# Eighteen batches of x rows, an earlier index load and a later far flag in a graph layer's edge loop

## The chip, the core and the metric

The kernel runs on one core of one Trainium2 chip. A core has a matrix engine (PE), a vector engine (VectorE, DVE in the profile), a scalar engine (ScalarE, ACT), GpSimd (POOL), a queue engine (SyncE, SP) and 16 DMA engines. The metric is the device time of one execution in microseconds. It is the median of several runs.

## The reference, cut to what matters

12500 nodes have rows x of 160 floats, 400000 edges have a source, a target (sorted by target), 16 and 4 attributes.

```python
h = jnp.maximum(_layernorm(x, axis=-1), 0.0)
# inside the layer, node_input is h, node_attr is node_vec1 (a)
s0 = x0 @ W_sc0 * a * inv0                 # skip path, 64 scalars
s1 = jnp.einsum('nuc,uv->nvc', x1, W_sc1) * a[:, :, None] * inv1
y0 = x0 @ W_l1_0 * a * inv0                # the rows that edges gather
y1 = jnp.einsum('nuc,uv->nvc', x1, W_l1_1) * a[:, :, None] * inv1
hid = jax.nn.silu(edge_length_embedded @ fc_W1 * (1.0 / math.sqrt(FC_IN)))
w = hid @ fc_W2 * (1.0 / math.sqrt(FC_H))  # 192 weights per edge, w_a w_b w_c w_d
ys0 = y0[edge_src]
ys1 = y1[edge_src]
mid_a = w_a * ys0 * e0                     # and mid_b, mid_c, mid_d: products of w, ys and e
z0 = jnp.zeros((n, MID), mid0.dtype).at[edge_dst].add(mid0) * inv_nb
z1 = jnp.zeros((n, MID, 3), mid1.dtype).at[edge_dst].add(mid1) * inv_nb
o0 = z0 @ W_l2_0 * a * inv_mid
o1 = jnp.einsum('nuc,uv->nvc', z1, W_l2_1) * a[:, :, None] * inv_mid
out = x + concat(C_S * s0 + C_X * o0, C_S * s1 + C_X * o1)
```

## The kernel before

**Node stage.** The nodes are 98 tiles of 128 rows, in groups of 2, then 8, and at the end 4 and 4. SyncE loads groups of x into `acc` (`load_x`, L322), which is also the accumulator of the output. Step q (two tiles) runs through `moments`, `center`, `turn_rows`, `out_of_psum`, `map_rows` and `leave`, each some steps later. ScalarE writes the rows y of a group into a buffer `ys` of the pool `ny` (two buffers), and SyncE stores it to `y_d` in DRAM. A buffer can be written again only when its store is done. On the engines the instructions stand in the order in which the code names them (a manual schedule), so an engine that waits holds up all that stands behind.

**Gathers.** An edge tile is 128 edges, a batch four tiles; there are 3125 tiles in 782 batches. For each tile GpSimd issues one indirect DMA that fetches 128 rows of y by the edges' sources (`gather`, L565). It can start only when all of `y_d` is stored. Batch b + 4's first gather is also held until the sums of batch b are done on PE, the third one of batch b + 3 until half of batch b's are (a dependency put in by hand, L576).

**Batches of x rows.** Every 16th batch, from batch 19 on, and 16 of them in all (`XB`), takes no rows from `y_d`. Its rows of x are gathered during the node stage (`x_fetch`, L345, into `xr`, by indices `xi` that `x_index` loads) and turned into rows of y in the edge loop (`hot`, `look_up`, `pick`, `x_center`, `x_turn`, `x_map`, `x_scale`). In the node stage each of these gathers is tied to an earlier step's `map_rows`.

**Edge loop.** For batch b: PE computes the edge weights two batches ahead (`weigh`, L599), VectorE the products of the next batch (`products`, L614, with a selection matrix `sel`), PE the sums over targets (`sums`, L626; four `pz` products per batch, two PSUM buffers that VectorE's transposes empty). A group of four windows then goes through `linear`, `add` and `accumulate` (L664, VectorE adds into `acc`). The list `waiting` holds up to two VectorE steps, which run at the start of the next batch (L867).

**Blocks.** Targets are related to windows in blocks of 24 batches (`relate`, L192, about twenty small VectorE steps). It also notes whether any edge lies outside its window; in the last block `any_far` (L239) reduces these notes, sums them on PE and writes the flag `far_i`. If it is set, a general path runs behind the loop.

**Skip work.** From batch 264 on (`SS`), every 10 batches (`SK`) two node tiles of x are loaded again, centred, transposed, multiplied by the skip weights and added to `acc`, 49 times.

**The end.** The last groups' stages follow one another, then the last eight tiles are stored, four by SyncE and four by ScalarE's queue; the very last has 84 rows and a store of its own.

Of the kernel before, what the change touches and what calls it, by code (L numbers as in the profile page):

```python
# [10 lines left out]
F32 = mybir.dt.float32  # L11
# [7 lines left out]
P = 128  # L19
M0 = 64  # L20
# [21 lines left out]
LATE = 8  # L42
XB = 16
SK = 10
LO = D - P
# [6 lines left out]
def kernel(  # L52
# [68 lines left out]
    assert GE > 0 and LOW > HN  # L121
    far_q = const.tile([P, NQ], F32, name="far_q")
    a_sb = const.tile([P, NT], F32, name="a_sb")
    look = const.tile([P, 2, NT], F32, name="look")
# [67 lines left out]
    def relate(rp, q):  # L192
# [44 lines left out]
        if n < size:  # L237
            nc.vector.memset(drel[:, n:size], 0.0)
    def any_far(rp, cnt):  # L239

        far = rp.tile([P, 1], F32, name="far")
        nc.vector.tensor_reduce(far, far_q, AX.X, ALU.max)
        nc.tensor.matmul(cnt, far, one, start=True, stop=True)
        nc.vector.tensor_scalar(far_i, cnt, 1.0, None, ALU.min)

    def node_weight_loads():
        nc.gpsimd.memset(wy0, 0.0)
        nc.gpsimd.memset(wyr, 0.0)
        nc.gpsimd.dma_start(wy0[0:M0, :], w_l1_0)
        for c in range(3):  # L250
            nc.gpsimd.dma_start(wyr[LO + c::3, M1 * c:M1 * (c + 1)], w_l1_1)

# [4 lines left out]
    def edge_zeros():  # L257
        nc.gpsimd.memset(ws0, 0.0)
        nc.gpsimd.memset(wsr, 0.0)
        nc.gpsimd.memset(w1, 0.0)  # L260
        nc.gpsimd.memset(wor, 0.0)
        if N % P:
            nc.gpsimd.memset(acc[:, NT - 1, :], 0.0)

# [41 lines left out]

    def node_dma(g, n, dma):

        f = min(g + n, N // P) - g
        if f:  # L310
            dma(slice(g * P, (g + f) * P), slice(0, f), P)
        if f < n:
            dma(slice((g + f) * P, N), slice(f, f + 1), N - (g + f) * P)

    def store(g, n, eng):
        node_dma(g, n, lambda rows, t, p: eng.dma_start(by_tile(out[rows, :]), acc[:p, g + t.start:g + t.stop, :]))

    def by_tile(ap):
        n = ap.shape[0]
        return ap.rearrange("(t p) c -> p t c", p=min(P, n))  # L320
# [11 lines left out]

    def x_index():
        t = x_batch(0) * GT
        nc.sync.dma_start(xi, src[:, t:t + XB * SB * GT].rearrange("p (u r) -> p u r", r=SB * GT)[:, :, 0:GT])

# [8 lines left out]
    def x_fetch(f, after):  # L345
        u, k = divmod(f, GT)
        fetch = nc.gpsimd.indirect_dma_start(  # L347
            out=xr[:, u, slot(k), :], out_offset=None, in_=x,
            in_offset=bass.IndirectOffsetOnAxis(ap=xi[:, u, k:k + 1], axis=0))
# [46 lines left out]
    with (  # L396
        tc.tile_pool(name="ny", bufs=2) as ny,
        tc.tile_pool(name="ns", bufs=4) as ns,
# [72 lines left out]

        LEAD = 5
        ready = ns.tile([P, 1], F32, name="ready")
        nc.scalar.activation(ready, eps, AF.Sqrt)
        node_weight_loads()
        edge_zeros()
        for i, (g, n) in enumerate(groups[:LEAD]):
            load_x(g, n)
            if i == 1:
                nc.sync.dma_start(a_sb, attr)  # L480
                x_index()
        last = len(steps) - 1
        more = list(groups[LEAD:])
        loads = edge_weight_loads()
        for q in range(len(steps) + 7):
            if q <= last and steps[q][2] == 0 and more:
                load_x(*more.pop(0))
            for f in range(4 * q // 3, 4 * (q + 1) // 3):
                if f < XB * GT:
                    x_fetch(f, mapped.get(q - 6))  # L490
            if q == 8:
# [21 lines left out]
            if q == last + 3:  # L513
# [3 lines left out]
                relate(rp, 0)  # L517
        assert 12 + len(loads) // 2 <= last and 3 * XB * GT <= 4 * (last + 8) and x_batch(XB) <= NB
    before.close()
# [16 lines left out]
    with (  # L536
# [257 lines left out]
        def extras(b):  # L794
# [35 lines left out]
            if u < XB and v in (3, 6):  # L830
                left(None)
                picked = look_up(u, HN * (v == 6))
                waiting[-1] = lambda: pick(u, HN * (v == 6), *picked)
            if r == KB - 13 and q + 1 < NQ:
                left(None)
                low_pt = p_x.tile([MW, P], F32, name="px")[:windows_in(q + 1), :]
                turn_low(q + 1, low_pt)
                waiting[-1] = lambda: most(q + 1, low_pt)
# [12 lines left out]
        for b in range(NB):  # L851
# [13 lines left out]
            if b + 1 < NB:  # L865
                products(b + 1)
            while waiting:  # L867
                waiting.pop(0)()
# [6 lines left out]
            if r == KB - 8 and q + 1 < NQ:  # L875
                relate(rp, q + 1)
                if q + 2 == NQ:
                    any_far(rp, p_x.tile([1, 1], F32, name="px"))
            if early and b > first_of[GE] + K - 1:
                store(*early.pop(0), nc.sync)  # L880
            sums(b)
            for m, part in ((b + AHEAD - 1, slice(2, GT)), (b + AHEAD, slice(0, 2))):
                if AHEAD <= m < NB and m not in xs_of:
                    gather(m, part)
            extras(b)
        while waiting:
# [163 lines left out]
```

## Time and profile before

| | us |
|---|---|
| median of 3 runs (3958.6 to 3969.82) | 3968.54 |
| profiled execution | 3957.18 |
| its span, first to last instruction | 3955.3 |
| GpSimd busy (3144 instructions) | 2963.8 |
| PE busy | 3583.4 |
| VectorE busy | 2747.0 |
| ScalarE busy | 615.2 |
| first gather starts (from x) | 7.77 |
| first gather from `y_d` starts | 94.68 |
| last gather starts | 3935.97 |

A row of a timeline gives start, time, engine, line, operation, result<-operands, how many were merged, and in brackets the engine's idle time before it and what ended it. SPq and ACTq are the DMA queues of SyncE and ScalarE. A row of a group gives count, busy time, mean time of one in ns, and behind the bar the idle time just before them.

### The profile page before, as it was taken

The page shows a single profiled execution, that of the slowest core. Times are in us where ns is not written, and L with a number is a line of the kernel's source. Part 1 is how long each engine was busy: PE and PEld are TensorE (multiplying, and loading weights), DVE is VectorE, ACT ScalarE, POOL GpSimd, SP SyncE. Part 2 cuts the span into 40 slices and gives each one's busy share as a digit, 9 for nine tenths or more (in the row PEclk, how much of TensorE's full clock was granted, in tenths as well). Part 3 has the DMA queues.
Part 4 walks back from the last instruction along what each step waited for, and adds up shares of the span by engine and source line. Part 5 has one row for each costly group of instructions (what it writes and reads, how often), then busy time and mean ns, then how long its engine had stood idle before and what let it go on. Part 6 is the DMA issues. An engine that isn't in the chain of part 4 may idle for free.

```text
span 3955.3 us, 54096 instructions
## 1 busy us (share of the span) xinstructions
PE 3583.4 (91%) x17202; PEld 2316.8 (59%) x17202; DVE 2747.0 (69%) x6877; ACT 615.2 (16%) x1845; POOL 2963.8 (75%) x3144
## 2 busy tenths in 40 slices
PE   7898899999999888898989989998999989999988
PEld 7555555555566555555555655555655556666655
DVE  7566666666667666666667777777777777777776
ACT  6111111111111111111111111111111111111111
POOL 6777777777777777777777777777777777777766
PEclk9999999999999999999999999999999999999989
DMA  8222222222222322222222232222223222223224
GB/s 233 72 77 78 74 78 76 76 77 73 77 77 76 81 79 78 78 81 79 81 78 79 76 83 78 81 78 74 81 79 83 77 80 77 81 79 83 75 81 124
DMA packets 262503, 329.05 MB, mean 83 GB/s; under 512 B 82888, under 2 KB 212216, under 8 KB 262216
## 3 DMA queue, kind: packets, MB, share of 16 engines
q0 software_dynamic: 150128, 256.23, 24.2%
q1 hardware_dynamic: 111590, 69.02, 6.2%
q8 instruction: 141, 2.31, 0.2%
q14 instruction: 146, 1.20, 0.1%
q10 hardware_dynamic: 498, 0.30, 0.0%
HBM read 307.67 MB, written 17.61 MB: 82 GB/s over the span
## 4 chain that ended last, share of the span: by engine, by line
PE 38%; DMA 23%; DVE 20%; issue 12%; POOL 7%; DVEq 1%; SPq 1%; ACT 0%; POOLq 0%; ACTq 0%
DMA yg<-y_d,src_q 22%; PE pz L636 20%; DVE pr L533 7%; PE pw L606 7%; POOL yg L571 7%; DVE pr L529 5%; PE px L585 4%; PE px L649 3%; DVE acc L672 1%; DVE za L642 1%; DVE za L643 1%; PE px L661 1%; DVE at L215 1%; DMA acc<-in_x 1%; DVEq L672 0%
## 5 line engine op out<-in xcount | busy, mean ns | idle before, releaser
L571 POOL DMA_INDIRECT yg<-y_d,src_q x3061 | 2897.9, 947 | 950.5 <-issue 636.7
L636 PE MATMUL pz<-pr,sel 128*128 128x320 f32 x6250 | 1972.0, 460 | 23.7 <-DVE za L643 23.7
L636 PEld LDWEIGHTS pz<-pr,sel 128*128 128x128 f32 x6250 | 1165.0, 196 | 606.7 <-issue 239.3
L529 DVE TENSOR_TENSOR pr<-pw,yg 128x512 f32<-128x512 f32 x766 | 527.8, 689 | 919.9 <-DMA yg<-y_d,src_q 919.1
L606 PE MATMUL pw<-w,hT 64*128 64x192 f32 x6250 | 733.8, 353 | 253.3 <-DVE pr L533 222.6
L606 PEld LDWEIGHTS pw<-w,hT 64*128 64x128 f32 x6250 | 505.5, 189 | 548.0 <-issue 372.2
L533 DVE TENSOR_TENSOR pr<-pw,yg 128x384 f32<-128x384 f32 x1532 | 774.0, 546 | 0.0
L622 DVE TENSOR_TENSOR sel<-own,pw 128x512 f32<-128x512 f32 x782 | 536.7, 686 | 27.0
L585 PE MATMUL px<-xe,w 32*128 32x512 f32 x782 | 439.1, 642 | 24.8 <-issue 21.4
L590 ACT ACTIVATE hT<-px 128x512 f32<-128x512 f32 x391 | 233.3, 597 | 1308.7 <-PE px L585 1308.7
L524 ACT ACTIVATE pw<-ev 128x20 f32<-128x20 f32 x782 | 149.1, 191 | 1381.6 <-PE pw L606 1219.2
L642 DVE STREAM_TRANSPOSE za<-pz 128x160 f32<-128x160 f32 x598 | 202.5, 339 | 169.4 <-PE pz L636 167.8
L649 PEld LDWEIGHTS px<-wo,za 128*128 128x128 f32 x1500 | 213.8, 192 | 118.7 <-issue 66.6
L649 PE MATMUL px<-wo,za 128*128 128x160 f32 x1500 | 245.1, 311 | 19.0 <-DVE high L182 8.1
L585 PEld LDWEIGHTS px<-xe,w 32*128 32x128 f32 x782 | 114.5, 183 | 200.7 <-issue 187.8
L643 DVE STREAM_TRANSPOSE za<-pz 32x160 f32<-32x160 f32 x598 | 202.1, 338 | 20.5
L620 DVE TENSOR_TENSOR own<-iota,pw 128x128 f32<-128x128 f32 x782 | 198.3, 254 | 13.7 <-ACT pw L524 10.1
L672 DVE SCALAR_TENSOR_TENSOR acc<-px,a_sb,acc 128x160 f32 x300 | 113.6, 379 | 9.5 <-PE px L661 3.9
L661 PE MATMUL px<-os,place 128*128 128x160 f32 x600 | 113.1, 311 | 7.7 <-DVE place L653 4.8
L661 PEld LDWEIGHTS px<-os,place 128*128 128x128 f32 x600 | 91.6, 192 | 42.2 <-issue 25.4
L651 ACT ACTIVATE os<-px 128x160 f32<-128x160 f32 x150 | 45.5, 303 | 253.1 <-PE px L649 253.1
L347 POOL DMA_INDIRECT xr<-in_x,xi x64 | 61.0, 953 | 21.9 <-issue 11.9
(128 smaller groups left out, 1312.7 us busy)
## 6 DMA issues: line engine op xcount, KB each, us to landing
yg<-y_d,src_q POOLq DMA_INDIRECT x3061
xe<-in_e SPq DMA_DIRECT2D x784, 32.0 KB
xs<-in_x SPq DMA_DIRECT2D x48, 160.0 KB
acc<-in_x SPq DMA_DIRECT2D x11, 640.0 KB
y_d<-ys SPq DMA_DIRECT2D x11, 640.0 KB
out<-acc SPq DMA_DIRECT2D x11, 640.0 KB
raw<-in_e SPq DMA_DIRECT2D x32, 192.0 KB
src_q<-in_src SPq DMA_DIRECT2D x32, 48.0 KB
```

The source lines that it names most:

```text
L529: nc.vector.tensor_mul(pr[:, :n, :].rearrange("p t (x u) -> p t x u", x=2)[:, :, :, 0:M0], wt[:, :n, 0:NW].rearrange("p t (x u) -> p t x u ...
L533: nc.vector.tensor_mul(pr[:, :n, D * x + M0:D * (x + 1)].rearrange("p t (c u) -> p t c u", c=3), wt[:, :n, 96 * x + M0:96 * (x + 1)].unsqu ...
L571: fetch = nc.gpsimd.indirect_dma_start(out=yg[:, slot(t), :], out_offset=None, in_=y_d, in_offset=bass.IndirectOffsetOnAxis(ap=ev4[t // BL ...
L585: nc.tensor.matmul(ph, w1[r, :], xe[r, :], start=True, stop=True)
L590: nc.scalar.activation(hT, ph, AF.Silu, scale=1.0 / math.sqrt(FC_IN))
L606: nc.tensor.matmul(pw[:, k, 0:NW], hT[r, o:o + P], w2[r, :], start=True, stop=True)
L622: nc.vector.tensor_tensor(sel, own[:, :n, :].unsqueeze(2).to_broadcast([P, n, 4, WN]), wt[:, :n, NW:NW + 4].unsqueeze(3).to_broadcast([P, ...
L636: mm = nc.tensor.matmul(pz[:, 0:PC], sel[:, slot(t), :, :], pr[:, slot(t), :], start=o == 0, stop=last)
L642: nc.vector.transpose(zT[g][:, :, at_w], pz[:, D:PC].rearrange("p (k u) -> p k u", k=ZK))
L643: nc.vector.transpose(zT[g][0:32, :, at_w], pz[0:32, 0:D].rearrange("p (k u) -> p k u", k=ZK))
L649: nc.tensor.matmul(po[:m, :], za[:, k, :m], wo[:, k, :], start=k == 0, stop=k == ZK - 1)
L661: nc.tensor.matmul(ps[:, h, :], place[:m, h, :], os[:m, :], start=True, stop=True)
```

## The change

1. `XB` goes from 16 to 18 and `SK` from 10 to 9; `SS`, which follows from `XB`, goes from 264 to 296. In the node stage 72 gathers from x stand where 64 did, and 3053 from `y_d` follow where 3061 did.
2. The indices of the first two batches of x rows are SyncE's first load, ahead of all loads of x. Those of the other 16 follow the second load of x.
3. The zeros of the weight tiles are written by VectorE and no longer by GpSimd, and four weight loads leave GpSimd's queue for ScalarE's.
4. The pool `ny` has three buffers.
5. `any_far` is cut into three: the reduction stays behind the last `relate`, PE's product comes two batches later, and the flag is written at the start of the batch after that.
6. In the last three batches (`K`) the waiting VectorE steps run behind the sums and not ahead of them.
7. In `store` the rows of the last, partial tile always go to SyncE's queue.

```diff
-XB = 16
-SK = 10
+XB = 18
+SK = 9
...
-    def any_far(rp, cnt):
-
-        far = rp.tile([P, 1], F32, name="far")
+    def most_far():
         nc.vector.tensor_reduce(far, far_q, AX.X, ALU.max)
+
+    def any_far(cnt):
         nc.tensor.matmul(cnt, far, one, start=True, stop=True)
+
+    def far_flag(cnt):
         nc.vector.tensor_scalar(far_i, cnt, 1.0, None, ALU.min)
 
     def node_weight_loads():
-        nc.gpsimd.memset(wy0, 0.0)
-        nc.gpsimd.memset(wyr, 0.0)
-        nc.gpsimd.dma_start(wy0[0:M0, :], w_l1_0)
+        nc.vector.memset(wy0, 0.0)
+        nc.vector.memset(wyr, 0.0)
+        nc.scalar.dma_start(wy0[0:M0, :], w_l1_0)
         for c in range(3):
-            nc.gpsimd.dma_start(wyr[LO + c::3, M1 * c:M1 * (c + 1)], w_l1_1)
+            nc.scalar.dma_start(wyr[LO + c::3, M1 * c:M1 * (c + 1)], w_l1_1)
...
     def edge_zeros():
-        nc.gpsimd.memset(ws0, 0.0)
+        nc.vector.memset(ws0, 0.0)
...
-    def node_dma(g, n, dma):
+    def node_dma(g, n, dma, rest=None):
...
-            dma(slice((g + f) * P, N), slice(f, f + 1), N - (g + f) * P)
+            (rest or dma)(slice((g + f) * P, N), slice(f, f + 1), N - (g + f) * P)
 
     def store(g, n, eng):
-        node_dma(g, n, lambda rows, t, p: eng.dma_start(by_tile(out[rows, :]), acc[:p, g + t.start:g + t.stop, :]))
+        def by(e):
+            return lambda rows, t, p: e.dma_start(by_tile(out[rows, :]), acc[:p, g + t.start:g + t.stop, :])
+        node_dma(g, n, by(eng), by(nc.sync))
...
-    def x_index():
+    def x_index(us):
         t = x_batch(0) * GT
-        nc.sync.dma_start(xi, src[:, t:t + XB * SB * GT].rearrange("p (u r) -> p u r", r=SB * GT)[:, :, 0:GT])
+        every = src[:, t:t + XB * SB * GT].rearrange("p (u r) -> p u r", r=SB * GT)[:, :, 0:GT]
+        nc.sync.dma_start(xi[:, us, :], every[:, us, :])
...
-        tc.tile_pool(name="ny", bufs=2) as ny,
+        tc.tile_pool(name="ny", bufs=3) as ny,
...
         LEAD = 5
+        x_index(slice(0, 2))
+        node_weight_loads()
         ready = ns.tile([P, 1], F32, name="ready")
         nc.scalar.activation(ready, eps, AF.Sqrt)
-        node_weight_loads()
         edge_zeros()
         for i, (g, n) in enumerate(groups[:LEAD]):
             load_x(g, n)
             if i == 1:
+                x_index(slice(2, XB))
                 nc.sync.dma_start(a_sb, attr)
-                x_index()
...
-            for f in range(4 * q // 3, 4 * (q + 1) // 3):
-                if f < XB * GT:
-                    x_fetch(f, mapped.get(q - 6))
+            for f in range(XB * GT * q // (last + 6), min(XB * GT * (q + 1) // (last + 6), XB * GT)):
+                x_fetch(f, mapped.get(q - 6))
...
+            if r == KB - 6 and q + 2 == NQ:
+                left(None)
+                cnt = p_x.tile([1, 1], F32, name="px")
+                any_far(cnt)
+                waiting[-1] = lambda: far_flag(cnt)
...
-            while waiting:
+            while waiting and b + K < NB:
                 waiting.pop(0)()
...
                 relate(rp, q + 1)
                 if q + 2 == NQ:
-                    any_far(rp, p_x.tile([1, 1], F32, name="px"))
+                    most_far()
...
             sums(b)
...
+            while waiting and b + K >= NB:
+                waiting.pop(0)()
             extras(b)
```

Here `last` is 48, so the x rows are spread as before, four gathers to three steps.

At the last `relate`, PE's order before: `px<-one,far` is the flag's product, `pw<-w,hT` the weights of a batch, `pz<-pr,sel` the sums of one, `px<-xe,w` the hidden layer of two, `px<-wo,za` and `px<-os,place` belong to a group's end.

```order
L636 MATMUL pz<-pr,sel 128x320 x4
L649 MATMUL px<-wo,za 128x160 x5
L606 MATMUL pw<-w_94,hT 128x192 x4
L243 MATMUL px<-one,far 1x1
L636 MATMUL pz<-pr,sel 128x320 x4
L585 MATMUL px<-xe,w_93 128x512
L661 MATMUL px<-os,place 128x160 x2
```

And now, from the same batch on:

```order
L642 MATMUL pz<-pr,sel 128x320 x4
L655 MATMUL px<-wo,za 128x160 x5
L612 MATMUL pw<-w_95,hT 128x192 x4
L642 MATMUL pz<-pr,sel 128x320 x4
L591 MATMUL px<-xe,w_94 128x512
L667 MATMUL px<-os,place 128x160 x2
L612 MATMUL pw<-w_95,hT 128x192 x4
L642 MATMUL pz<-pr,sel 128x320 x4
L612 MATMUL pw<-w_95,hT 128x192 x4
L642 MATMUL pz<-pr,sel 128x320 x4
L591 MATMUL px<-xe,w_94 128x512
L655 MATMUL px<-wo,za 128x160 x5
```

The flag's product no longer stands ahead of the first batch's sums; it follows behind the last of these rows, ahead of the next batch's weights:

```order
L655 MATMUL px<-wo,za 128x160 x5
L244 MATMUL px<-one,far 1x1
L612 MATMUL pw<-w_95,hT 128x192 x4
L642 MATMUL pz<-pr,sel 128x320 x4
L667 MATMUL px<-os,place 128x160 x2
```

In VectorE's order at the end, before, the last full batch's products (`pr`) are followed by a group's addition (`acc`), then by the transposes (`za`) and the last, single tile (`own`):

```order
L533 TENSOR_TENSOR pr<-pw,yg 128x4x96 x2
L667 TENSOR_LOAD tile_i
L672 ISA x2
L672 SCALAR_TENSOR_TENSOR acc<-px,a_sb,acc 128x160
L672 ISA x2
L672 REGISTER_ALU
L672 SCALAR_TENSOR_TENSOR acc<-px,a_sb,acc 128x160
L642 STREAM_TRANSPOSE za<-pz 128x5x32
L643 STREAM_TRANSPOSE za<-pz 32x5x32
L642 STREAM_TRANSPOSE za<-pz 128x5x32
L643 STREAM_TRANSPOSE za<-pz 32x5x32
L620 TENSOR_TENSOR own<-iota,pw 128x32
```

Now the addition stands between the transposes and the single tile:

```order
L539 TENSOR_TENSOR pr<-pw,yg 128x4x96 x2
L648 STREAM_TRANSPOSE za<-pz 128x5x32
L649 STREAM_TRANSPOSE za<-pz 32x5x32
L648 STREAM_TRANSPOSE za<-pz 128x5x32
L649 STREAM_TRANSPOSE za<-pz 32x5x32
L673 TENSOR_LOAD tile_i
L678 ISA x2
L678 SCALAR_TENSOR_TENSOR acc<-px,a_sb,acc 128x160
L678 ISA x2
L678 REGISTER_ALU
L678 SCALAR_TENSOR_TENSOR acc<-px,a_sb,acc 128x160
L626 TENSOR_TENSOR own<-iota,pw 128x32
```

The same instructions stand there; four transposes moved ahead of the addition.

More of the change, by code (lines that the diff above doesn't have):

```diff
@@ L122 @@
     far_q = const.tile([P, NQ], F32, name="far_q")
+    far = const.tile([P, 1], F32, name="far")
     a_sb = const.tile([P, NT], F32, name="a_sb")
@@ L257, in edge_zeros @@
     def edge_zeros():
-        nc.gpsimd.memset(ws0, 0.0)
-        nc.gpsimd.memset(wsr, 0.0)
-        nc.gpsimd.memset(w1, 0.0)
-        nc.gpsimd.memset(wor, 0.0)
+        nc.vector.memset(ws0, 0.0)
+        nc.vector.memset(wsr, 0.0)
+        nc.vector.memset(w1, 0.0)
+        nc.vector.memset(wor, 0.0)
         if N % P:
-            nc.gpsimd.memset(acc[:, NT - 1, :], 0.0)
+            nc.vector.memset(acc[:, NT - 1, :], 0.0)
     def edge_weight_loads():
@@ L517 @@
                 relate(rp, 0)
-        assert 12 + len(loads) // 2 <= last and 3 * XB * GT <= 4 * (last + 8) and x_batch(XB) <= NB
+        assert 12 + len(loads) // 2 <= last and x_batch(XB) <= NB
     before.close()
```

## The prediction

> **What bounds the kernel now.** I read the page first (busy time, the chain that ended last, the costliest groups), then GpSimd's timeline, then the places where its even step breaks, then the stages by windows. On the page PE looks like the bound and the chain names many lines:
>
> ```profile
> PE 3583.4 (91%) x17202; PEld 2316.8 (59%) x17202; DVE 2747.0 (69%) x6877; ACT 615.2 (16%) x1845; POOL 2963.8 (75%) x3144
> PE 38%; DMA 23%; DVE 20%; issue 12%; POOL 7%; DVEq 1%; SPq 1%; ACT 0%; POOLq 0%; ACTq 0%
> L571 POOL DMA_INDIRECT yg<-y_d,src_q x3061 | 2897.9, 947 | 950.5 <-issue 636.7
> L529 DVE TENSOR_TENSOR pr<-pw,yg 128x512 f32<-128x512 f32 x766 | 527.8, 689 | 919.9 <-DMA yg<-y_d,src_q 919.1
> L347 POOL DMA_INDIRECT xr<-in_x,xi x64 | 61.0, 953 | 21.9 <-issue 11.9
> ```
>
> The groups say otherwise. VectorE spends 919 us waiting for gathered rows, and GpSimd's two kinds of gather fill 2897.9 + 950.5 + 61.0 + 21.9 = 3931.3 us with their own time and the gap before each. GpSimd's timeline shows what a gap is:
>
> ```profile
> 98.43 0.94 POOL L571 DMA_INDIRECT yg<-y_d,src_q  x1 [0.30 <-issue]
> 99.68 0.95 POOL L571 DMA_INDIRECT yg<-y_d,src_q  x1 [0.30 <-issue]
> ...
> 7.77 1.02 POOL L347 DMA_INDIRECT xr<-in_x,xi  x1 [2.12 <-DMA xi<-in_src]
> ...
> 3935.97 0.95 POOL L571 DMA_INDIRECT yg<-y_d,src_q  x1 [0.30 <-PE pz L636]
> ```
>
> A gather takes 0.95 and the next follows after 0.30, so one goes out every 1.25 us. From the first (7.77) to the last (3935.97) are 3928.2 us for 3124 steps; at 1.25 these are 3905.0, and 23.2 us are left for every wait that GpSimd has in the whole run. So GpSimd's gathers are the bound, at one fixed price each, and their number (3125) does not change: a batch of x rows has four gathers from x in place of four from y_d. The change can win only in the 7.8 us ahead of the first gather, in the 23.2 us of waits, and in the 19.3 us behind the last. The three large waits are these:
>
> ```profile
> 87.58 0.95 POOL L347 DMA_INDIRECT xr<-in_x,xi  x1 [0.30 <-issue]
> 94.68 0.94 POOL L571 DMA_INDIRECT yg<-y_d,src_q  x1 [6.16 <-DMA xe<-in_e]
> ...
> 3843.82 0.94 POOL L571 DMA_INDIRECT yg<-y_d,src_q  x1 [3.74 <-PE pz L636]
> ...
> 3853.33 0.94 POOL L571 DMA_INDIRECT yg<-y_d,src_q  x1 [4.82 <-PE pz L636]
> ```
>
> Less the 0.30 of every step they are 5.86, 3.44 and 4.52 us, 13.8 of the 23.2.
>
> **Two more batches of x rows, started earlier.** Rows of x can be gathered before y_d is stored, rows of y_d only behind its last store. Before, 64 gathers lie ahead of that point and 3061 behind it; now 72 and 3053. The 8 gathers save 8 x 1.25 = 10.0 us behind the point, if the point stays. It stays only if 72 gathers fit ahead of it, and that hangs on when the first starts:
>
> ```profile
> 0.75 0.96 SPq L323 DMA_DIRECT2D acc<-in_x  x2
> 2.38 0.43 SPq L335 DMA_DIRECT2D xi<-in_src  x1
> 3.14 0.55 DVE L411 BATCH_NORM_STATS2 st<-acc 128x6 f32<-128x160 f32 x2 [2.23 <-DMA acc<-in_x]
> 1.57 0.13 POOL L105 IOTA lane<- 128x1 f32 x1
> 4.70 0.78 POOL L261 MEMSET wor<- 128x800 f32 x1
> ```
>
> The indices now go first, in 256 pieces. The load that stood in that place, also of 256 pieces, was issued at 0.75 and used at 3.14. GpSimd, whose memsets and weight loads are gone, is free at 1.70. I take 3.4 for the first gather: 3.14 and a quarter for GpSimd to see it. The ends are 3.0 and, if the load is no faster than the old one, 7.8. From 3.4, 72 steps of 1.25 end at 93.4; with 0.6 for waits on the row maps that pace them the first gather from y_d could go at 94.0. The last store of y_d is the other condition:
>
> ```profile
> 60.18 0.68 ACT L466 ACTIVATE ys<-po,look 128x160 f32<-128x160 f32 x2 [5.67 <-DMA y_d<-ys]
> ACT ys L466 <- DMA y_d<-ys: 16.0, 6, 5.7
> 91.73 0.42 SPq L468
> ```
>
> That store was issued at 91.73, and by the 2.4 us of the first load it was there at 94.1; the gather followed at 94.68. The third buffer takes away what made ScalarE wait six times for a store, 16.0 us in all; I expect several us less in the node stage, against 0.5 us later x loads (one index load ahead on SP) and four weight loads on ScalarE's queue, at GpSimd's price for them (735 and 517 ns each) about 2.3 us, ahead of its first real work at 6.8. So I take 94.2 for the first gather from y_d: 10.0 + 0.5 = 10.5 us won. Ends: 10.7, and 6.7 if the node stage (unshortened and 1.5 late) or the first gather (7.8) sets it near 98. The second index load has 16-byte pieces as before and ten us until the ninth gather needs it.
>
> VectorE's seven memsets cost GpSimd 0.14 to 0.78 us each. VectorE has 2.2 us free there; its 256 columns of L653 take 0.30:
>
> ```profile
> L653 DVE TENSOR_SCALAR place<-iota,at x150: 299/300/585, 223.3 to 3946.6; 128x256 f32<-128x256 f32 x150
> ```
>
> so 1408 columns are about 1.7 us, from 0.9 to 2.6, ahead of the rows at 3.6. Nothing is paid.
>
> [...]
>
> **The far flag.** Before, the flag's matmul stands on PE ahead of a batch's sums and waits for the whole relation of the last block on VectorE:
>
> ```profile
> 3835.82 0.17 DVE L199 TENSOR_REDUCE first<-negb 128x5 f32<-128x20 f32 x1
> ...
> 3840.92 0.19 PE L243 MATMUL px<-one,far 128*1 128x1 f32 x2 [8.94 <-DVE far L242]
> 3841.04 4.64 PE L636 MATMUL pz<-pr,sel 128*128 128x320 f32 x8
> ...
> 3850.56 3.87 PE L636 MATMUL pz<-pr,sel 128*128 128x320 f32 x8
> ...
> 3855.20 2.42 PE L636 MATMUL pz<-pr,sel 128*128 128x320 f32 x8
> ```
>
> PE stood for 8.94 us, the sums came late, and the gathers, which keep step with them, waited 3.44 and then 4.52 us. Moved two batches on, the matmul finds its operand ready; queued behind it there is a weighing, not sums. The relation itself (5 us of VectorE, 3835.82 to 3840.92) stays, as at the other blocks. The largest of the other waits of a gather behind PE's sums were these:
>
> ```profile
> 423.80 0.95 POOL L571 DMA_INDIRECT yg<-y_d,src_q  x1 [1.19 <-PE pz L636]
> ...
> 3254.90 0.94 POOL L571 DMA_INDIRECT yg<-y_d,src_q  x1 [1.30 <-PE pz L636]
> ```
>
> 0.9 and 1.0 over the step; I leave 0.7 here, so 7.96 - 0.7 = 7.2 us won. Is the second wait, 4.52, a child of the first? After the stand eight matmuls took 4.64 and 3.87 us, and 2.42 once running again, so PE was slow for ten us and the second wait came out of that. TensorE: Matmul & The Clock Gate, of the Trainium skill, in Part 1, says that about 3.4 us of an idle PE halve its clock; by it both waits go, the trace agrees (4.64 against 2.42), and the sum stands. Were the second wait of its own making, 2.7 would be won here. Ends: 7.96 and 2.7.
>
> **The end.** The addition of a group on VectorE (0.80 us) moves behind the next batch's four transposes, which free PE's sums:
>
> ```profile
> 3938.95 0.80 DVE L672 SCALAR_TENSOR_TENSOR acc<-px,a_sb,acc 128x160 f32 x2
> 3940.52 2.39 PE L636 MATMUL pz<-pr,sel 128*128 128x320 f32 x8 [3.16 <-DVE za L643]
> 3942.41 0.35 DVE L642 STREAM_TRANSPOSE za<-pz 128x160 f32<-128x160 f32 x1 [0.52 <-PE pz L636]
> 3949.83 0.38 SPq L316 DMA_DIRECT2D out<-acc  x1
> 3949.85 2.43 ACTq L316 DMA_DIRECT2D out<-acc  x2
> SPq L1046 <- DMA out<-acc: 4.1, 1, 4.1
> ```
>
> PE could start 0.8 earlier, but VectorE, with the same work to do, had only 0.52 of idle time ahead of the next transpose: 0.5 us won. The last rows' store leaves ScalarE's queue, where two stores took 2.43 us, for SP's (0.38): half of 2.43 less to issue, 1.2 us. Together 1.7; ends 0.4 and 2.5.
>
> **What it costs.** 32 more batches lie in the stage with x rows, and the skip work comes every 9 batches, not 10. The stages (node stage, x rows, skip work) stand so now:
>
> ```profile
> core 0: us, PE busy (x) PEld busy (x) DVE busy (x) ACT busy (x) POOL busy (x), PEclk, DMA share, GB/s
> 0.00:95.00 95.00, 74.03 (x596) 71.56 (x598) 70.37 (x363) 63.65 (x171) 66.16 (x84) 0.93 0.86 236
> 95.00:1340.00 1245.00, 1133.32 (x5348) 712.67 (x5346) 815.37 (x1869) 209.24 (x615) 939.67 (x992) 0.98 0.28 77
> 1340.00:3820.00 2480.00, 2263.22 (x10748) 1459.15 (x10748) 1771.19 (x4409) 328.55 (x1014) 1875.48 (x1982) 0.97 0.29 79
> POOL yg L571 <- PE pz L636: 68.7, 190, 4.8
> ```
>
> PE is 91% busy in both, but GpSimd hardly waits for it: of 68.7 us in 190 gaps, 57.0 are the 0.30 of each and 7.96 the far flag's; 3.7 us are left. If all of them fell in the 264 batches up to 1340, 32 more would add 0.5 us. I take 0.5; ends 0 and 3 (nearly all again).
>
> **Sum.** 10.5 + 7.2 + 1.7 - 0.5 = 18.9 us won. The profiled execution took 3957.18 us (its span 3955.3 and 1.9 around it), so 3938.3 against it. The median of the runs shown is 3968.54, 11.4 above it; 18.9 off that gives **3949.6 us**, 0.48% less. A measurement of this kernel tells about 0.3% from no change, 11.9 us.
>
> **The rivals.**
> - *The node stage sets the start.* The stores of y_d, not the x rows, come last, and the third buffer only lets loads and stores collide sooner. For it: the DMA engines are busiest there, a share of 0.86 in the first row of the windows against 0.28 and 0.29. The point then lies near 98, not 94.2, and the gain is 15.1: 3953.4. Against it: 16.0 us of waits that lose their cause.
> - *The indices are not early.* The small load lands no sooner than 7.8; 72 gathers end at 98.4: gain 14.7, 3953.8. Against it: a load in the same place was used at 3.14.
> - *PE takes over where x rows are.* If the 32 batches run at 5.0 us each with the x work on PE, the 8 gathers are saved in vain: gain 8.9, 3959.6, within 0.3%. For it: PE 91%. Against: 3.7 us of waits.
> - *Slower: the clock.* The skip work is denser by a ninth. PE's 2263 us at a granted clock of 0.97 fill 2480 at 0.885; below that PE is the bound there. To end 12 us slower it must take back 31: 2511 us, a clock under 0.874 over the whole stage. For it: 0.97 is not 1. Against: the slow stretches follow idle PE and do not sum to a load. It would give 3980.5.
>
> **Chances.** Forecast 0.68, node stage 0.11, indices 0.08, PE 0.08, clock 0.05. The first three lie over 0.3% faster, 0.87; of these I move 0.06 to within, since the runs shown differ by 11 us. So faster 0.81, within 0.14 (0.08 and 0.06), slower 0.05. The ends of the terms: 10.7 + 7.96 + 2.5 - 0 = 21.2, and 6.7 + 2.7 + 0.4 - 0.5 = 9.3 (with the 3 added, 6.8). Low: 21.2 off the lowest run shown, 3958.6: 3937. High: 3960, which takes in the first three rivals.
>
> **What would show it.** Right: first gather near 3.4; gathers from x and y_d in one row with no gap over 2 us near 94; no gap over 1.5 us beside the far matmul, and that matmul waiting under 1 us; steps of 1.25 throughout; 17 to 18 us behind the last gather. Wrong: a step over 1.26, a gap of several us at the first gather from y_d, or gaps in every skip period.

## The result, and the profile after

| | before | changed |
|---|---|---|
| median of 6 runs, us | 3966.88 (3958.6 to 3969.82) | 3951.1 (3948.13 to 3952.74) |
| ratio | | 0.996, 95% interval 0.995 to 0.997 |
| profiled execution (its span), us | 3957.18 (3955.3) | 3949.02 (3947.1) |

The changed kernel is faster by 0.4%, 15.8 us between the medians. The forecast was 3949.6. The two profiled executions differ by 8.2 us only; the gathers say why.

The page of the changed kernel, busy times and the two groups of gathers:

```profile
PE 3586.2 (91%) x17274; PEld 2318.0 (59%) x17274; DVE 2750.7 (70%) x6898; ACT 622.3 (16%) x1863; POOL 2969.1 (75%) x3133
L577 POOL DMA_INDIRECT yg<-y_d,src_q x3053 | 2899.0, 950 | 933.2 <-issue 651.8
L353 POOL DMA_INDIRECT xr<-in_x,xi x72 | 69.1, 960 | 25.2 <-issue 14.0
```

GpSimd's gathers and the gaps ahead of them are still nearly the whole span: 3926.5 of 3947.1 us. There are 8 fewer from `y_d`, yet their busy time has not fallen (2897.9 before, 2899.0 now): a gather took 950 ns on average where it took 947. So the time of the last gather is best written as a sum, start of the first + 3124 steps + waits. The step is the mean distance of neighbouring gathers under 1.3 us apart; every longer distance counts as a wait with what it has over that mean. Made this way, the parts always add up to the last gather; what they tell is where the time lies.

| us | first gather | step, ns | waits among gathers from x | wait at the first gather from `y_d` | waits at the far flag | all other waits | last gather |
|---|---|---|---|---|---|---|---|
| before | 7.77 | 1250.2 | 1.02 | 5.86 | 7.95 | 7.76 | 3935.97 |
| changed | 2.83 | 1253.1 | 3.24 | 0 | 0 | 6.44 | 3927.18 |

Waits and start together are 17.9 us less (30.4 and 12.5). The step took 2.9 ns x 3124 = 9.1 us of that back in this pair of traces. Whether that is the change's doing is taken up at the end.

The start, in the timelines of SyncE, GpSimd and VectorE:

```profile
0.76 0.48 SPq L341 DMA_DIRECT2D xi<-in_src  x1
2.26 0.19 DVE L266 MEMSET acc<- 128x160 f32 x1
2.83 1.10 POOL L353 DMA_INDIRECT xr<-in_x,xi  x1 [1.15 <-DMA xi<-in_src]
4.04 0.55 DVE L417 BATCH_NORM_STATS2 st<-acc 128x6 f32<-128x160 f32 x2 [1.59 <-DMA acc<-in_x]
14.06 0.94 POOL L353 DMA_INDIRECT xr<-in_x,xi  x1 [1.23 <-PE po L462]
16.57 0.94 POOL L353 DMA_INDIRECT xr<-in_x,xi  x1 [1.57 <-PE po L462]
```

The indices let the first gather go at 2.83. The last of VectorE's memsets ended at 2.45, ahead of it. But at 14.06 and 16.57 the gathers wait for PE's `po`, the row maps to which each is tied: the early start has run ahead of its own pace.

The point where `y_d` must be ready, on SyncE's queue and GpSimd:

```profile
60.09 26.23 SPq L474 DMA_DIRECT2D y_d<-ys  x9
95.02 0.95 POOL L353 DMA_INDIRECT xr<-in_x,xi  x1 [0.30 <-issue]
96.27 0.95 POOL L577 DMA_INDIRECT yg<-y_d,src_q  x1 [0.30 <-issue]
```

The last store of `y_d` was issued at 85.8 (91.73 before), the 6.16 gap has gone, and the gathers themselves now set this point, at 96.27 and not at 94.2.

The place of the far flag, on PE and on GpSimd:

```profile
3846.86 1.12 PE L591 MATMUL px<-xe,w 32*128 32x512 f32 x2
3847.91 1.63 PE L655 MATMUL px<-wo,za 128*128 128x160 f32 x10
3849.47 0.19 PE L244 MATMUL px<-one,far 128*1 128x1 f32 x2
3849.59 0.92 PE L612 MATMUL pw<-w,hT 64*128 64x192 f32 x8
POOL yg L577 <- PE pz L642: 54.1, 172, 0.9
```

The flag's matmul has no wait where it stood 8.94 us before. The last row, from the list of waits, gives 172 gaps behind PE's sums with none over 0.9 us.

The end, on GpSimd, PE, VectorE and the two store queues:

```profile
3927.18 0.94 POOL L577 DMA_INDIRECT yg<-y_d,src_q  x1 [0.30 <-issue]
3930.92 3.95 PE L642 MATMUL pz<-pr,sel 128*128 128x320 f32 x8 [2.70 <-DVE za L649]
3931.70 0.80 DVE L678 SCALAR_TENSOR_TENSOR acc<-px,a_sb,acc 128x160 f32 x2 [0.33 <-issue]
3940.58 0.81 DVE L678 SCALAR_TENSOR_TENSOR acc<-px,a_sb,acc 128x160 f32 x2 [1.53 <-PE px L667]
3941.92 1.64 SPq L320 DMA_DIRECT2D out<-acc  x2
3943.33 0.40 ACTq L320 DMA_DIRECT2D out<-acc  x1
```

PE's sums start 3.73 us behind the last gather (4.55 before), since the addition on VectorE now comes after. But the eight matmuls took 3.95 us where the row of before has 2.39, and 19.9 us lie behind the last gather, where 17 to 18 were forecast and 19.3 stood before.

### The profile page after: what moved, and what is told of

It is laid out like the page before. It is cut to its first block, busy times and chain, and to the rows that moved or that the text cites. A ratio compares the mean times of both kernels' runs of the same rounds, so it can differ in the third digit from the quotient of the medians.

```text
span 3947.1 us, 54257 instructions
## 1 busy us (share of the span) xinstructions
PE 3586.2 (91%) x17274; PEld 2318.0 (59%) x17274; DVE 2750.7 (70%) x6898; ACT 622.3 (16%) x1863; POOL 2969.1 (75%) x3133
## 4 chain that ended last, share of the span: by engine, by line
PE 34%; DMA 24%; DVE 19%; issue 13%; POOL 9%; DVEq 1%; SPq 0%; ACT 0%; POOLq 0%; ACTq 0%
DMA yg<-y_d,src_q 23%; PE pz L642 17%; POOL yg L577 9%; DVE pr L539 7%; PE pw L612 7%; DVE pr L535 5%; PE px L591 4%; PE px L655 2%; DVE acc L678 1%; DVE za L648 1%; DVE at L216 1%; DVE za L649 1%; PE px L667 1%; PE po L462 0%; PE px L749 0%
## 5 line engine op out<-in xcount | busy, mean ns | idle before, releaser
L577 POOL DMA_INDIRECT yg<-y_d,src_q x3053 | 2899.0, 950 | 933.2 <-issue 651.8
L626 DVE TENSOR_TENSOR own<-iota,pw 128x128 f32<-128x128 f32 x782 | 198.3, 254 | 13.3 <-ACT pw L530 9.7
L353 POOL DMA_INDIRECT xr<-in_x,xi x72 | 69.1, 960 | 25.2 <-issue 14.0
```

The costliest lines, as they stand in the source:

```text
L577: fetch = nc.gpsimd.indirect_dma_start(out=yg[:, slot(t), :], out_offset=None, in_=y_d, in_offset=bass.IndirectOffsetOnAxis(ap=ev4[t // BL ...
```

## The experiments

They ran on three chips, called A, B and C here, four on each in the order of this section. The kernel before had a median of 3957.99 us on A and 3965.03 on C. The changed kernel itself was not run on A, so what a part left out there is worth is read from the waits and not from the time. The runs on these two, taken apart as above; the first column names what is in the kernel:

| us | first gather | step, ns | among x | first from `y_d` | far flag | other | last gather |
|---|---|---|---|---|---|---|---|
| before, again | 7.76 | 1250.2 | 0.59 | 7.46 | 4.14 | 8.01 | 3933.73 |
| all but far later | 2.90 | 1250.3 | 3.79 | 0 | 4.47 | 10.70 | 3927.64 |
| all but 18 batches | 2.98 | 1250.3 | 3.37 | 2.92 | 0 | 7.59 | 3922.88 |
| all but third buffer | 2.90 | 1250.3 | 5.53 | 0 | 0 | 8.26 | 3922.54 |
| all, gathers from x paced looser | 2.92 | 1252.1 | 0.68 | 2.08 | 0 | 6.64 | 3923.89 |
| all, again | 2.94 | 1252.1 | 4.20 | 0 | 0 | 11.57 | 3930.41 |
| all but early indices | 8.09 | 1250.2 | 0.30 | 0 | 0 | 9.41 | 3923.48 |
| all but order at the end | 2.94 | 1252.1 | 5.79 | 0 | 0 | 7.18 | 3927.42 |

**Before, again.** No edit.

> The kernel before, profiled a second time. In the two profiles GpSimd's undisturbed step (start of one gather to the next) was 1.2502 us before and 1.2531 after; over 3124 steps that is 9.1 us. Theory: the step belongs to the execution and not to the kernel, so here it may lie anywhere from 1.250 to 1.254, and the time is 3957 plus 3124 times what it is above 1.2502; the waits of GpSimd come again to about 22.5 us (5.9 at the first gather from y_d, 3.4 and 4.5 at the far flag) and about 19.3 us lie behind the last gather. Rival: the change made the step longer; then it is 1.250 again here and the time 3957.

3959.19 us. The waits are there again, at other sizes: 7.46 for 5.86 at the first gather from `y_d`, and at the far flag 4.14 for 7.95. The end was 23.7 us long, 4.3 longer than in the first profile of the same kernel. The step is 1250.2 ns again, as the rival has it.

**The far flag back in its old place.**

```diff
-            if r == KB - 6 and q + 2 == NQ:
...
-                waiting[-1] = lambda: far_flag(cnt)
...
                 # behind most_far()
+                    cnt = p_x.tile([1, 1], F32, name="px")
+                    any_far(cnt)
+                    far_flag(cnt)
```

> The changed kernel with the far flag's product put back directly behind the last relation of a block, ahead of a batch's sums. Theory: PE stands there for about 9 us again, the two waits of GpSimd of 3.4 and 4.5 us come back, its waits grow from 9.7 to 17 or 18 us and the time by 7 to 8 us. Rival 1: only the first wait is the flag's, plus 3.4. Rival 2: gathers run far enough ahead, no wait, plus 0 to 1.

3945.83 us, ratio 0.9971 (0.9958 to 0.9983). PE's timeline and GpSimd's gaps at that place:

```profile
3836.14 0.19 PE L244 MATMUL px<-one,far 128*1 128x1 f32 x2 [8.85 <-DVE far L241]
3836.26 4.61 PE L642 MATMUL pz<-pr,sel 128*128 128x320 f32 x8
3843.44 2.42 PE L642 MATMUL pz<-pr,sel 128*128 128x320 f32 x8
3839.03 0.94 POOL L577 DMA_INDIRECT yg<-y_d,src_q  x1 [3.75 <-PE pz L642]
3845.06 0.94 POOL L577 DMA_INDIRECT yg<-y_d,src_q  x1 [1.33 <-DVE za L649]
```

The stand (8.85) and the first wait (3.75 - 0.30 = 3.45) return as they were. The second wait is 1.03: here PE's next sums took 2.42 us, while in the profile of before they were still slow (3.87) and the wait was 4.52. None of the seven traces with the flag in its new place has such a pair of waits, so the second wait comes with the first. Its size goes with how long PE's clock stays low. Two rows of the windows, of before and of this run, with the granted clock third from the end:

```profile
3836.45:3853.51 17.06, 12.59 (x30) 7.26 (x31) 8.60 (x34) 0.79 (x2) 6.78 (x8) 0.50 0.29 84
3830.48:3840.72 10.24, 4.58 (x10) 2.60 (x10) 7.05 (x32) 0.00 (x0) 5.17 (x6) 0.50 0.17 43
```

Half the clock was granted for 17.06 us in before, until the second wait was over, and for 10.24 us here and in the second trace of before, ending ahead of that wait: it was 4.52, 1.03 and 0.70 us.

**Sixteen batches, all else changed.**

```diff
-XB = 18
-SK = 9
+XB = 16
+SK = 10
...
-            for f in range(XB * GT * q // (last + 6), min(XB * GT * (q + 1) // (last + 6), XB * GT)):
-                x_fetch(f, mapped.get(q - 6))
+            for f in range(4 * q // 3, 4 * (q + 1) // 3):
+                if f < XB * GT:
+                    x_fetch(f, mapped.get(q - 6))
```

> The changed kernel with 16 batches of x rows and skip work every 10 batches, as before, paced as before (four gathers in three steps). Theory (gathers are the bound, and what counts is only whether GpSimd stands still at the first gather from y_d): 64 gathers end near 86, the stores of y_d are there near 89, so GpSimd stands 2 to 4 us and the time grows by that. Rival: each gather ahead of y_d is a gain by itself, 8 x 1.25, so plus 10 us.

3943.39 us, ratio 0.9961 (0.9947 to 0.9975), the same ratio as the whole change has on another chip. The two extra batches do not show in the time; the interval, 11 us wide, could not show 2.92 us. GpSimd's timeline shows what they are worth:

```profile
85.12 0.95 POOL L353 DMA_INDIRECT xr<-in_x,xi  x1 [0.31 <-issue]
89.29 0.94 POOL L578 DMA_INDIRECT yg<-y_d,src_q  x1 [3.23 <-DMA xe<-in_e]
```

With 64 gathers from x the point lies at 89.29 and GpSimd stands 2.92 us there. Eight more gathers in front of it fill that stand and push the point 7 to 10 us back; all that can be won by them is the 2.92.

**Two buffers for the rows of y.** `bufs=3` to `bufs=2` in the pool `ny`.

> The changed kernel with two buffers of y rows, as before. Theory: ScalarE waits for stores again (16 us before), the last store of y_d is issued near 92 and is there near 94.5, still ahead of 96.3, where the x gathers end: the first gather from y_d stays within 0.5 us of 96.3 and the time is the same. Rival: the third buffer is needed for 18 batches; then the first gather from y_d comes at 98 or later with a wait in front of it, plus 2 us or more.

3942.75 us, one run. The last store of `y_d` is issued at 90.6 (85.8 to 88.6 in the runs with 18 batches, three buffers and the old pace), so the buffer does shorten the node stage by 2 to 5 us. But no gap appears ahead of the first gather from `y_d`, because the 72 gathers end later still, at 98.46. What grows is the wait of gathers from x on the row maps, 5.53 us, and that varies as much with no edit at all there (3.24, 3.79, 4.20, 5.79).

**Four kernels on chip B.** The next four ran where the kernel before took 4619.26 us, 16% more than elsewhere.

Indices of all batches behind the second load of x:

> The changed kernel with the indices in one load behind the first two loads of x and the attributes, as before. Theory: the first gather comes at 8 to 11 and not 2.9; the pacing waits (2.4 to 4.2) disappear under that, so the first gather from y_d comes at 98.5 to 101, 2 to 5 us later, and so does the end. Rival 1: the whole delay of 5 us or more reaches the end. Rival 2: nothing does, since the stores of y_d set that gather.

The additions of finished groups ahead of the sums to the end:

> The changed kernel with the waiting VectorE steps of the last three batches back ahead of the sums. Theory: PE's next sums start 4.5 us behind the last gather and not 3.8, the last addition ends 13.3 us behind it and not 12.6 (both about 1.6 or more later if PE runs at half clock there), time plus 0.7. Rival: the new order lets PE start on a half clock (14.2 in the profile of the change); with the old order no such stretch comes and the last addition ends at 13.3, time minus 0.9.

Gathers from x tied to the row maps of two batches of steps earlier (`mapped.get(q - 8)` for `mapped.get(q - 6)`):

> The changed kernel with each gather of x rows tied to the row maps of eight steps earlier, not six. Theory: the 2.4 to 4.2 us that GpSimd waited at its 9th to 11th gather are the pacing's alone; they go, the first gather from y_d comes at 93 to 94 and not 96.3 to 98.5, the time falls by 2 to 4 us. Rival: gathers that run ahead collide with the loads of x, the stores of y_d come last, and GpSimd waits in front of its first gather from y_d: no gain, or a loss of a few us.

The changed kernel, no edit:

> The changed kernel unchanged, again. Theory (the step between gathers belongs to the execution): with a step of 1.2503, as in the four other profiles taken since, 9 to 11 us of GpSimd's waits and 18.3 to 20.4 us behind the last gather, 3938 to 3942 us, 15 to 19 less than the kernel before. Rival: the step of 1.2531 belongs to the changed kernel: 3949 again. If the last gather is followed by a half-clock stretch of PE within 6 us, the additions end 14.2 us behind it, if not 12.6.

They took 4614.94, 4600.22, 4606.98 (ratio 0.9974, 0.9956 to 0.9992) and 4607.36 us (0.9969, 0.9954 to 0.9985). The step of the gathers is 1252.9 ns in the changed kernel there, but waits of GpSimd sum to 662 us, all through the run. GpSimd, ScalarE and the windows of the changed kernel on that chip:

```profile
2408.88 0.95 POOL L577 DMA_INDIRECT yg<-y_d,src_q  x1 [0.31 <-issue]
2412.46 0.95 POOL L577 DMA_INDIRECT yg<-y_d,src_q  x1 [2.63 <-remote]
2412.07 0.30 ACT L657 ACTIVATE os<-px 128x160 f32<-128x160 f32 x1 [7.39 <-remote]
core 0: us, PE busy (x) PEld busy (x) DVE busy (x) ACT busy (x) POOL busy (x), PEclk, DMA share, GB/s
100.00:2000.00 1900.00, 1603.14 (x7010) 1005.80 (x7010) 1077.84 (x2508) 264.00 (x806) 1240.70 (x1304) 0.91 0.27 67
```

ScalarE stood 7.39 us with its operand there, and VectorE, PE and GpSimd went on right behind it; the trace names no cause in the core's own program ("remote" is another core or an unknown queue, and no wait of that kind stands in any of the ten traces of the two tables). The granted clock is 0.91 from 100 to 2000 us (0.98 in the first trace of the changed kernel). The runs carry some 660 us of waits that the expectations do not know, so most of the numbers expected of them cannot be read there. With the late indices the first gather from `y_d` came 2.4 us later than in the changed kernel (118.08 and 115.67), inside the 2 to 5 of the theory. The change is worth 0.3% there too. All four kernels ran again on chip C.

**The pace of the gathers from x.** The edit of `mapped.get` above.

> The changed kernel with each gather from x paced by the row maps of two batches earlier (q - 8 for q - 6), on a chip whose gathers run undisturbed. Theory (the pacing waits of 2.4 us at the 9th to 11th gather are real losses, since every later gather starts that much later and nothing else ends later): no wait on the row maps, first gather from y_d at 93.1 to 94.0 (96.28 in the changed kernel) without a wait in front of it, last gather 2.3 to 3.2 earlier at an equal step, time 2 to 3 us below the changed kernel's in the same job. Rival (the slack is taken by the first gather from y_d, whose rows are not there yet): the wait moves in front of the first gather from y_d, which stays near 96, time the same within 1 us.

3947.67 us, ratio 0.9955 (0.9941 to 0.9968). GpSimd's timeline, and the list of its waits in the first 100 us:

```profile
92.56 0.97 POOL L353 DMA_INDIRECT xr<-in_x,xi  x1 [0.30 <-issue]
95.89 0.95 POOL L577 DMA_INDIRECT yg<-y_d,src_q  x1 [2.36 <-DMA xe<-in_e]
POOL xr L353 <- PE po L462: 3.7, 12, 0.4
```

The rival is right about the point, and the theory about the time, 3.3 us below the changed kernel's next to it. The waits on the row maps are gone (0.4 the longest), and two microseconds of them stand ahead of the first gather from `y_d` instead: the last store of `y_d` was issued at 90.6 here, 87.7 in the next run. The point moved to 95.89, 1.4 earlier than in that run, which is of the changed kernel.

**The changed kernel, again.** No edit.

> The changed kernel as it is, beside the loose pace and the kernel before on the same chip. If the step of 1.2531 us between gathers in its first profile belongs to that execution, this one shows 1.250 or 1.253 with no relation to the kernel, and the time is 14 to 18 us below the kernel before. If the change itself lengthens the step, it is 1.253 again while the kernel before shows 1.250.

3950.94 us, ratio 0.9961 (0.9948 to 0.9975), 14.1 us below the kernel before. The step is 1252.1 ns: nearer to the rival's 1.253 us than to the 1250.2 ns of the kernel before, of which there is no trace on this chip. The looser pace is 3.3 us below it by the medians, with 1.4 of that at the first gather from `y_d`. In the two traces its other waits are 4.9 us fewer as well (6.64 and 11.57), but these scatter as much between runs of other kernels, so the rest is not accounted for. The waits on the row maps stand in its timeline:

```profile
14.40 0.94 POOL L353 DMA_INDIRECT xr<-in_x,xi  x1 [1.59 <-PE po L462]
16.91 0.94 POOL L353 DMA_INDIRECT xr<-in_x,xi  x1 [1.56 <-PE po L462]
19.42 0.94 POOL L353 DMA_INDIRECT xr<-in_x,xi  x1 [1.57 <-PE po L462]
```

**Late indices.**

```diff
-        x_index(slice(0, 2))
...
             if i == 1:
-                x_index(slice(2, XB))
                 nc.sync.dma_start(a_sb, attr)
+                x_index(slice(0, XB))
```

> The changed kernel with the indices loaded after the first rows of x, as before the change. Theory: the first gather starts near 7.8 us instead of 2.84, and since the waits on the row maps (2.4 to 3.2 us) then fall away, the first gather from y_d comes 1.7 to 2.6 later than in the changed kernel (98.0 to 98.9), not 4.9 later: of the early start some 2 us is worth something. Rival (each microsecond of start counts whole): first gather from y_d 4.9 later, near 101.

3945.32 us in one run, not slower than the whole change; against the changed kernel on this chip 5.9 us of that are its step (1250.2). GpSimd's timeline at the start and at the point:

```profile
8.09 1.10 POOL L353 DMA_INDIRECT xr<-in_x,xi  x1 [6.40 <-DMA xi<-in_src]
98.36 0.95 POOL L576 DMA_INDIRECT yg<-y_d,src_q  x1 [0.30 <-issue]
```

The first gather is 5.2 us later, the first from `y_d` 1.1 to 2.1 later than in the two runs of the changed kernel, with 1.7 to 2.6 in the theory and 4.9 in the rival: the waits on the row maps shrink to 0.30.

**The old order at the end.**

```diff
-            while waiting and b + K < NB:
+            while waiting:
                 waiting.pop(0)()
...
-            while waiting and b + K >= NB:
-                waiting.pop(0)()
```

> The changed kernel with the additions of finished groups ahead of the sums at every batch, as before the change. Theory: the first sum on TensorE after the last gather starts at 4.5 us behind it instead of 3.8, and the last addition ends 0.7 to 0.8 later than in a run of the changed kernel with the same clock behind the last gather (13.3 for 12.6 without a stretch of half clock, 15.0 for 14.2 with a short one). Rival (the order of the additions is worth nothing because the last group's own sums end last): equal within 0.2.

3950.4 us in one run. PE's first sums and VectorE's last addition behind the last gather (3927.42):

```profile
3931.93 3.63 PE L642 MATMUL pz<-pr,sel 128*128 128x320 f32 x8 [3.42 <-DVE za L649]
3941.58 0.80 DVE L678 SCALAR_TENSOR_TENSOR acc<-px,a_sb,acc 128x160 f32 x2 [1.52 <-PE px L667]
```

The sums start 4.50 behind the gather and the addition ends 14.96 behind it; in the other run of the changed kernel on this chip it is 3.82 and 14.28. So the order is worth 0.7 us in this pair, as expected, both with a stretch of slow matmuls.

## Why the prediction was right, and where its steps were not

**The bound: right.** One gather per step, 3125 of them, set the last gather in every run of the two tables: start and waits together are 12.3 to 30.4 us of some 3930 there, and the steps all the rest. PE did not take over: the gaps behind its sums (54.1 us in 172, against 68.7 in 190) have not grown, and the granted clock from 1340 to 3820 us is 0.97 as before: the rivals of PE and of the clock fall. The node stage does not set the start in the changed kernel, since no gap stands there.

**The start: right in sign, 10.5 forecast, about 8 measured.** First gather, waits among x and wait at `y_d` add up to 14.7 and 15.8 before, and to 6.1, 6.7, 7.1 and 8.7 in the four runs that have this part of the change whole: 15.2 - 7.2 = 8.0 us. The first gather came even sooner (2.83 for 3.4). The failed term is "0.6 for waits on the row maps that pace them": they took 3.2 to 5.8 us. The start and the pace were costed apart, though each gather from x is tied to a row map, so that one which starts sooner only waits sooner. The same runs tell that the three parts overlap: without the 18 batches the three terms add up to 9.3, without the third buffer to 8.4, without the early indices to 8.4. Each part alone is thus worth 1 to 2 us on top of the other two, of the size of the scatter. "10.0 us for 8 gathers" named the wrong owner: the number of gathers is fixed, so 8 of them placed ahead of the point win only the time for which GpSimd stood there.

**The far flag: mechanism right, size from one draw.** The wait and its child went as forecast, 7.2 us. The first wait is 3.44 in three of three runs with the old place; the second was 4.52, 0.70 and 1.03. Their sums are 7.95, 4.14 and 4.47, 5.5 on the mean. The lower end 2.7 was meant for a second wait with a cause of its own; the runs show it small where the half clock ended sooner, after 10.24 us and not 17.06. Between the ratios, 0.9971 without this part and 0.996 with it on another chip, it is about 4 us, less than the intervals can separate.

**The end: order right, store mis-sized, clock left out.** The order gave 0.7 (0.5 forecast). The store gave 0.3 and not 1.2: from the last addition to the end of the span are 6.03 and 6.25 us before and 5.68 to 6.09 in the eight runs with the new stores, 5.88 on the mean, and the ranges overlap. The step that failed is "half of 2.43 less to issue". The 84-row store is slow on SyncE too, as the row of 1.64 us for two shows, and ScalarE's single store now begins later (3943.33, 1.9 us behind the addition). And the matmuls behind the last gather run slow in seven of the ten traces of the tables: in before, sixteen batches and two buffers they don't. With a short slow stretch the last addition ends 14.2 to 14.3 us behind the last gather (new order), without one 12.6 (new order) or 13.3 (old). The profile of before was one of the three lucky ones, so 17 to 18 was its luck carried over. TensorE: Matmul & The Clock Gate, of the Trainium skill, in Part 1, calls the window of the clock gate free-running, which would make it a matter of phase. The traces agree. Two windows behind the last gather, of the changed kernel and then of sixteen batches, with PE's busy time second and the granted clock third from the end:

```profile
3928.19:3931.60 3.41, 0.71 (x4) 0.56 (x4) 2.78 (x7) 0.00 (x0) 0.00 (x0) 1.00 0.09 24
3931.60:3935.01 3.41, 3.41 (x9) 2.23 (x8) 2.60 (x10) 0.00 (x0) 0.00 (x0) 0.50 0.01 2
3922.39:3925.80 3.41, 1.57 (x6) 0.76 (x4) 1.59 (x4) 0.00 (x0) 1.13 (x2) 1.00 0.20 50
3925.80:3929.21 3.41, 2.50 (x11) 1.90 (x12) 2.95 (x13) 0.00 (x0) 0.00 (x0) 1.00 0.01 2
```

In each trace the granted clock changes at points that lie a multiple of 3.41 us apart. PE was idle for nearly the same time in both kernels, 2.70 and 2.75 us. In the changed kernel all of that fell between two such points, and the next 3.41 us had half the clock; in sixteen batches it was split between two stretches, 1.84 and 0.90, and the clock stayed. In all seven traces with a slow stretch PE idled for 2.0 to 3.4 of the 3.41 us ahead of it, in the other three for 1.84 at most. That is no sharp bound: over the ten traces, from 14 us on, more than 2.0 us was always followed by half the clock, and 0.8 to 2.0 us sometimes.

**The cost: right.** All other waits of GpSimd are 7.8 us on the mean with 16 batches (7.76, 8.01, 7.59) and 8.6 with 18 (6.44 to 11.57); 0.5 was forecast. The scatter is larger than the difference.

**The sum.** 8.0 + 5.5 + 0.7 + 0.3 - 0.8 = 13.7 us at an equal step, against 18.9 forecast and 15.8 and 14.1 between the medians of two pairs. That the forecast came so near, 3949.6 for 3951.1, is partly luck: two of its terms, the start and the store, were too large, the far flag's was the upper of its three draws, and "steps of 1.25 throughout" was taken as given. The base helped too: 3968.54 had become 3966.88 with three more runs, and against that 15.8 of the 18.9 us came. Against the profiled run 3938.3 was forecast and 3949.02 came: 9.1 of these 10.7 us are the step.

**The step: the traces speak against my theory.** I took it to belong to an execution. The changed kernel, late indices, looser pace and old order were each traced on B and on C, the changed one once more and the kernel before twice, and each kept its side. The views of one line, with the count, and the least, median and largest time of a gather in ns, are those of the kernel before, of the changed kernel (its first run, then on B and C) and of the kernel with late indices (on C and B):

```profile
L571 POOL DMA_INDIRECT yg<-y_d,src_q x3061: 940/946/1292, 94.7 to 3936.0; - x192
L577 POOL DMA_INDIRECT yg<-y_d,src_q x3053: 942/949/1348, 96.3 to 3927.2; - x191
L577 POOL DMA_INDIRECT yg<-y_d,src_q x3053: 943/949/1432, 115.7 to 4579.6; - x191
L577 POOL DMA_INDIRECT yg<-y_d,src_q x3053: 942/947/1332, 97.3 to 3930.4; - x191
L576 POOL DMA_INDIRECT yg<-y_d,src_q x3053: 942/946/1348, 98.4 to 3923.5; - x191
L576 POOL DMA_INDIRECT yg<-y_d,src_q x3053: 940/946/1342, 118.1 to 4591.9; - x191
```

The changed kernel had 1253.1, 1252.9 and 1252.1 ns, the one with late indices 1250.2 on chip C and 1249.7 on chip B, where the changed one had the second and third of its values, B's first. So in the traces it goes with the program, and by the medians of one gather (946 ns against 947 to 949) it lies in the gather's own time, not in the gap of 0.30 us. Which part it goes with is open. On B and on C the three kernels with the early indices have the longer step and the one without them the shorter, as in the first pair. On A three kernels with the early indices have the shorter one: either the part that each leaves out (far flag, 18 batches, third buffer) matters as well, or every kernel has the shorter step on that chip. The changed kernel was not traced on A, so this rival stands. In the medians the 6 to 9 us don't show: with them the change would be worth 5 to 8 us, and it is worth 14 to 16. The kernel before had a median 9.7 us above its traced execution beside the first run of the changed kernel (3966.88 for 3957.18), and on chip A about that of its trace (3957.99 for 3959.19). On C one of its nine runs took 3956.9 us and the others 3961.73 to 3968.08. A longer step in some executions of the same kernel would do that, and would speak for my theory after all, but these have no trace.

**Left open.** What sets the step, whether it goes with the early indices or with the chip, and whether the change lengthens it in untraced executions too; why the looser pace gains 3.3 us where its point moved by 1.4; what stops the engines on chip B. Putting the looser pace, or 16 batches, together with a short step on one chip wasn't tried.

## What to carry to other kernels

Where one engine issues a fixed number of equal instructions, write its end as first start + number x step + waits: up to the last of them nothing that isn't in one of the three can win, and parts of a change that aim at the same wait are not added up. Ask of an earlier start what paces the instructions behind it, and of a wait read in one profile whether a second execution has it at the same size. Compare two kernels by the waits in their traces and by many timed runs; the difference of two profiled times may be all step.

## What the runs showed of the hardware

The distance of gathers that wait for nothing is constant within an execution but not between the traces: 1250.2 or 1250.3 ns in six of the ten traces of the tables, 1252.1 in three, 1253.1 in one. Over 3124 steps that is up to 9 us, as much as the largest part of this change, with the same instruction, rows and sizes.

A chip on which everything took 16% longer kept GpSimd's own price (1249.7 to 1253.0 ns in four kernels). What came on top were 659 to 680 us of waits, with the other engines standing for microseconds at the same time. The granted clock was 0.90 to 0.91 there, against 0.97 to 0.98 in the other traces.

An 84-row store of 54 KB took longer to issue than one of four full tiles, 1.0 to 1.7 us against 0.38 on SyncE, and changing the queue it goes to moved the end by 0.3 us on the mean.

The clock granted to PE changed only at points a multiple of 3.41 us apart: the half-clock stretches named here lasted 3.41, 10.24 and 17.06 us. Wherever PE had idled for more than 2.0 us between two neighbouring points half the clock followed; after 0.8 to 2.0 us it sometimes did. So about 2.7 us of idle PE behind the last gather cost 1.7 us in one execution and nothing in another.
